# One shared last pass: the fourth kan of the last two units as a pair with full rows, and their stores on two DMA queues

## The chip, the cores and the metric

The kernel runs on one core of a Trainium2 chip. The metric is the device time of one execution, in microseconds (us). The core has a matrix engine (PE), a vector engine (DVE), a scalar engine (ACT) that evaluates functions, a general engine (POOL), and a synchronising engine (SP) that here issues DMAs. DMAs are issued from SP, ACT or POOL into a queue of that engine and carried out by 16 DMA engines. Work on the engines runs side by side; each engine takes its own instructions strictly in the order in which they were written.

## What is computed

The input x is 16 images of 32 channels of 128 x 128 in float32. There are two layers, each a group norm followed by a block whose result is added to its input:

```python
x = x + _L0_conv_ref(_gn(x), ...)     # layer 0: attention over channels, heads are 8 images
x = x + _L1_conv_ref(_gn(x), ...)     # layer 1: windows of 8 x 8, four "fastkan" layers

def _fastkan(x, ln_g, ln_b, ws, wb, bb):
    ln = _layernorm(x, ln_g, ln_b)
    basis = jnp.exp(-((ln[..., None] - GRID) / DENOM) ** 2)      # 8 bumps per value
    return basis.reshape(...) @ ws.T + jax.nn.silu(x) @ wb.T + bb
# in layer 1, y = _layernorm(windows):
a = _fastkan(y seen along the rows, k1...)
d = _fastkan(y seen along the columns, k2...)
e = _fastkan(y, k3...)
z = _fastkan(a + d + e, k4...)
out = z + wins
```

The fourth kan (k4) works on the sum of the first three, so for one piece of the image it can't begin before the third is complete.

## The kernel before

**Units.** Layer 0 needs sums over whole images: the kernel first loads x, turns it on DVE (L658) and sums a Gram matrix on PE (L684). From it `attention` works out one small matrix per half of the batch (L697 to L974). After that, layer 0 is only a matrix product per piece. The image is cut into 64 units of 128 partitions x 1024 values, numbered n = 0 to 63 (N = 64). Layer 1 is done unit by unit.

**Passes.** The four kans are run in pairs, since a kan fills only half of a tile that is 2048 values wide. Pass a of unit n holds kan 1 and kan 2 of that unit. Pass b of unit n holds kan 3 of unit n in its first half and kan 4 of unit n - 2 (BACK = 2) in its second half. Weights and norm scales lie accordingly: in `wt_b` (L418) and `back["b"]` (L416) the upper 64 partitions hold k3 and the lower 64 hold k4, and likewise in the columns `par_b` (L327), built in `parameters` (L486 to L585) at the start from 8 DMAs on POOL's queue (L508) and small operations on DVE. Since kan 4 lags by two, pass b is run N + BACK = 66 times. In passes 64 and 65 there is no kan 3 left, so `norm_b` (L1266) puts the one z into both halves; kan 3's half of the result is thrown away.

One pass is a chain:
- `norm`: 16 matmuls subtract the mean (L1110 through `tiled`, L436), ACT copies to SBUF (L1115, two halves), squares (L1118), PE averages (L981), ACT makes the inverse root (L983, L984), PE spreads it over the partitions (L1123).
- `scale`: DVE multiplies, two halves (L1140).
- `seed`: ACT makes the first bump (L1149, L1154) and two ratios R, up and down (L1151, L1157).
- `ladder`: DVE makes the other seven bumps by multiplying with R, one after the other in each direction (L1169, seven operations).
- `products`: PE multiplies each bump with its weights, 16 matmuls of 32 x 32 at a time (L436), sums them in a pair of PSUM tiles X, and adds the silu blocks (L1205; `silus`, L1300, after the fourth bump) and, for kan 3, the results of kans 1 and 2 (L1314 to L1331).

Kan 3's sum is copied out by ACT as z (`evict_z`, L1251), and ACT makes its silu (`silus`, L1068, L1083, with a load of the function table before, and another after at L1084). Kan 4's sum is added to the unit's input by DVE (`result`, L1351), which needs the unit's xh loaded again (`again`, L1370), and `store` (L1355 to L1364) writes it by four DMAs on SP's queue. The columns and the rows are exchanged between kans by DMAs on SP's queue too: `move` (L1098, `d<-yy`) and `move_back` (L1241).

**What sets the order.** The functions named above are generators. A small planner, `Flow` (L87 to L236), runs them when the kernel is built. It knows each step's engine, an assumed cost and the buffers that the step takes, and writes out the instructions in the order in which it would start them. For the steady part the order on each engine is written out by hand (`ORDER`, L53 to L74, a list of step names with the distance in units); the start, before the second Gram matrix is complete, and the tail are left to the planner's assumed times. Tiles come from pools with few buffers (L450 to L471; two xh, two z, two X, two Y), so a step can also wait for a buffer.

Of the kernel before, what the change touches and what calls it, by code (L numbers as in the profile page):

```python
# [10 lines left out]
F32 = mybir.dt.float32  # L11
AF = mybir.ActivationFunctionType
ALU = mybir.AluOpType
# [6 lines left out]
P = 128  # L20
NG = 8
NT = NG + 1
# [23 lines left out]
LAG = 0.2  # L46
LANDING = 2.5
PATIENCE = 3.0
BACK = 2
# [190 lines left out]
def conv_preact_kernel(  # L240
# [75 lines left out]
    def column():  # L316
        used[0] += 1
        return vec[:, used[0] - 1 : used[0]]
# [6 lines left out]

    par_a = [column() for _ in range(4)]
    par_b = [column() for _ in range(4)]  # L327


    quad = const.tile([P, 4], F32, name="quad")  # L330
# [82 lines left out]
        )  # L413


    back = {name: const.tile([P, P], F32, name=f"back_{name}") for name in ("0", "a", "b")}  # L416
    wt_a = const.tile([P, NT, 32], F32, name="wt_a")
    wt_b = const.tile([P, NT, 32], F32, name="wt_b")  # L418

    silu_a = [const.tile([P, P], F32, name=f"silu_a{k}") for k in range(2)]  # L420
    silu_b = [const.tile([P, P], F32, name=f"silu_b{k}") for k in range(2)]
# [22 lines left out]
    def layers():  # L444
        with ExitStack() as es:
# [40 lines left out]
            def parameters():  # L486

                yield "get", "projections"
                raw, = yield step("POOL", 85.0, "sz")
                back_t = raw[:, 0:384].rearrange("p (k q m) -> p k q m", k=3, q=4)  # L490
                st_a = [
                    raw[:, 384 + k * NT * 16 : 384 + (k + 1) * NT * 16].rearrange("p (t n) -> p t n", t=NT)
                    for k in range(2)
                ]
                st_b = [raw[:, 704 + k * 32 : 736 + k * 32] for k in range(2)]
# [9 lines left out]
                for q in range(4):  # L505
                    for s in range(2):
                        at = q * 32 + s * 16
                        nc.gpsimd.dma_start(  # L508
                            out=wt_b[at : at + 16, :, :], in_=(w3 if q < 2 else w4)[s * 64 : s * 64 + 16]
                        )  # L510
                        for k, src in enumerate((w3, w4)):
                            nc.gpsimd.dma_start(
                                out=st_b[k][at : at + 16, :], in_=src[s * 64 : s * 64 + 16, NG, :]
                            )
# [4 lines left out]
                for par, top, bottom in (  # L519
                    (par_a, (c1["k1_g"], c1["k1_b"]), (c2["k2_g"], c2["k2_b"])),  # L520
                    (par_b, (cr["k3_g"], cr["k3_b"]), (cr["k4_g"], cr["k4_b"])),
                ):
                    g, bq, bp_, bn = par
                    yield step("DVE", 0.8)
                    for o, (mine_g, mine_b) in ((slice(0, 64), top), (slice(64, 128), bottom)):
                        TS(g[o, :], mine_g[o, :], INV_DENOM, None, ALU.mult)
                        TS(bq[o, :], mine_b[o, :], INV_DENOM, 0.5, ALU.mult, ALU.add)
                        TS(bp_[o, :], mine_b[o, :], 2.0 * INV_DENOM, None, ALU.mult)
                        TS(bn[o, :], mine_b[o, :], -2.0 * INV_DENOM, None, ALU.mult)
                for k, (name, groups, scale) in enumerate(  # L530
                    (
                        ("0", quad, cr["pn_g"]),
                        ("a", group8.rearrange("p q j -> p (q j)"), par_a[0]),
                        ("b", quad, par_b[0]),
                    )
                ):
                    n = 8 if name == "a" else 4
                    t = back_t[:, k]
                    yield step("DVE", 0.2)
                    TS(t[:, :, 0:n], groups.unsqueeze(1).to_broadcast([P, 4, n]), scale, None, ALU.mult)  # L540
                    ps_, = yield step("PE", 0.4, "Y")
                    nc.tensor.transpose(ps_[:, 0, 0:P], t.rearrange("p q m -> p (q m)"), ident)
                    yield step("DVE", 0.3)
                    nc.vector.tensor_copy(back[name], ps_[:, 0, 0:P])
                    give("Y")


                for k in range(2):
# [20 lines left out]
                        group8[:, :, 1].unsqueeze(2).unsqueeze(3).to_broadcast([P, 4, 2, 8]),  # L569
                        ALU.mult,  # L570
                    )
                yield step("DVE", 0.45)
                TT(wt_b, wt_b, fac.unsqueeze(2).to_broadcast([P, NT, 32]), ALU.mult)
                for k in range(2):
                    yield step("DVE", 0.5)
# [529 lines left out]
            def norm(name, n, wt, rhs, e, then):  # L1105
# [11 lines left out]
                sq, = yield step("ACT", 1.81, "u")  # L1117
                ACT(sq, v, AF.Square)  # L1118
                lr = yield from rsqrt_rows(sq, P, e, 4, "lr")
                give("u")  # L1120
                rb = yield step("PE", 1.1, "Y", "Y")
                for q in range(4):
                    MM(  # L1123
                        rb[q // 2][:, q % 2, :],
                        lhsT=back[name][32 * q : 32 * q + 32, :],
                        rhs=lr[32 * q : 32 * q + 32, :],
                        start=True,
                        stop=True,
                    )
# [125 lines left out]
            def norm_a(n):  # L1255
# [7 lines left out]
                    lambda: used(("d", n), "d", 2),  # L1263
                )

            def norm_b(n):  # L1266
                y = z = None
                if n < N:
                    y = yield "get", ("yy", n)
                if n >= BACK:  # L1270
                    z = yield "get", ("z", n - BACK)
                rows = lambda t, h: t[:, 4 * h : 4 * h + 4, 0, :]
                cols = lambda t, h: t[:, 512 * h : 512 * h + 512]
                two = (y, rows) if n < N else (z, cols), (z, cols) if n >= BACK else (y, rows)

                def then():
                    if n < N:
                        used(("yy", n), "yy", 3)
                    if n >= BACK:
                        used(("z", n - BACK), "z", 2)  # L1280

                yield from norm(
                    "b",
                    n,
                    c32,
                    lambda g_, q: two[q // 2][1](two[q // 2][0], q % 2)[32 * g_ : 32 * g_ + 32],
                    e4m,
                    then,
                )

            def pair_b(n):
# [3 lines left out]

                def bank(acc, at, rows, k, h):
                    to = acc[k][at : at + rows, h, :]
                    return to.rearrange("p (h n w) -> p h w n", h=4, w=8) if k else to

                def silus(acc):  # L1300
                    for k, (key, m) in enumerate((("s", n), ("sz", n - BACK))):
                        if 0 <= m < N:
                            t = yield "get", (key, m)
                            yield step("PE", 1.06, lag=0.0)
                            cols = lambda h, o: t[o, 512 * h : 512 * h + 512]
                            third = lambda h, o: cols(h, o).rearrange("p (h w n) -> p h w n", h=4, w=8)
                            blocks(
                                lambda h: silu_b[k],
                                third if k else cols,
                                lambda h, f: bank(acc, 64 * ((f + h) % 2), 64, k, h),  # L1310
                            )
                            used((key, m), key, 1)

                def adds(acc):  # L1314
                    ar = yield "get", ("ad", n)
# [17 lines left out]
                also = {2: silus}  # L1333
                if n < N:
                    also[5] = adds
                acc = yield from products("b", n, wt_b, also, (0, 2, 0, 2), bank)
                if n < N:
                    put(("z_acc", n), acc[0], LAG)
                else:
                    give("X")  # L1340
                if n >= BACK:
                    put(("last", n - BACK), acc[1], LAG)
                else:
                    give("X")

            def result(n):
# [8 lines left out]
            def store(n):  # L1355
                bp, kk, j = units[n]
                xh = yield "get", ("result", n)
                yield step("SP", 2.6, lag=0.0)
                for b in range(4):
                    nc.sync.dma_start(  # L1360
                        out=out_rows[bp * KK + kk, b, :, :, j * RB : (j + 1) * RB], in_=xh[32 * b : 32 * b + 32, :]
                    )
                late = fl.moved(1.4, 2.0)
                give("xh", late)  # L1364
# [5 lines left out]
                nc.sync.dma_start(out=xh, in_=xd)  # L1370
                put(("again", n), xh, fl.moved(1.4))

            both = [("b", n) if b else ("a", n) for n in range(N + BACK) for b in range(2) if b or n < N]
            one = lambda name, task: [(name, 0, task)]
            every = lambda name, task, units=N: ((name, n, task(n)) for n in range(units))
            with tc.manual_schedule(engines=IN_ORDER):
# [10 lines left out]
                        every("evict_z", evict_z),  # L1387
                        every("result", result),
                        every("again", again),
                        every("scale_b", lambda n: scale("b", n), N + BACK),  # L1390
                        every("scale_a", lambda n: scale("a", n)),
                        ((f"seed_{k}", n, seed(k, n, par_a if k == "a" else par_b)) for k, n in both),
                        every("norm_b", norm_b, N + BACK),
                        every("norm_a", norm_a),
                        every("silus", silus, N + LATE),
                        every("move_back", move_back),
# [92 lines left out]
```

## Time and profile before

| what | us |
|---|---|
| median of 3 runs | 2868.09 (2866.86 to 2873.42) |
| the profiled execution | 2870.64 |
| its span, from first to last instruction | 2868.9 |
| PE busy | 2746.1 (96%) |
| DVE busy | 2685.3 (94%) |
| ACT busy | 2517.7 (88%) |
| POOL busy | 53.8 (2%) |
| the last operation on DVE (`result` of unit 63, L1351) ends | 2854.9 |

The span divides into a start up to some 330 us (loads, Gram matrices, attention, the first units), a steady stretch in which a unit follows a unit, and a tail. Groups of instructions that matter here: the ladder, L1169, 910 operations of 2286 ns; the products, L436, 605 ns for a matmul record, several of which run beside each other on parts of the array; L1140, 260 of 1216 ns; L1115, 260 of 1015 ns; L1118, 1905 ns; L1149 to L1157, 1901 to 1996 ns each; the eviction of z, L1251; the stores, 256 DMAs of 128 KB on SP's queue. A name such as `u<-R,u` in these views gives the tile written and the tiles read. "PEclk" or "granted clock" is the share of its full clock that PE was granted in a stretch.

### The profile page before, as it was taken

What the parts mean: (1) busy time and instruction counts of PE and PEld (TensorE: products, weight loads), DVE (VectorE), ACT (ScalarE), POOL (GpSimd) and SP (SyncE); (2) the same over time, 40 slices, a digit from 0 to 9 for tenths busy, and PEclk for the clock granted to TensorE, in tenths of its full rate; (3) what the DMA queues carried; (4) which work ended last, traced back from release to release, by engine and by line L of the source; (5) the groups of instructions that cost most, each with busy time, mean ns of one, the idle gap of its engine ahead of it and who ended that gap; (6) DMA issues with size and microseconds to landing.
All of it is one profiled execution on the core that took longest, in us unless ns stands there. A gap on an engine that the chain in (4) does not pass through costs nothing.

```text
span 2868.9 us, 100690 instructions
## 1 busy us (share of the span) xinstructions
PE 2746.1 (96%) x45955; PEld 1091.5 (38%) x45955; DVE 2685.3 (94%) x1793; ACT 2517.7 (88%) x2035; POOL 53.8 (2%) x109
## 2 busy tenths in 40 slices
PE   6999999999999999999999999999999999999985
PEld 6874433333333333333333333333333333333321
DVE  4747999999999999999999999999999999999986
ACT  0026899999999999999999999999999999999973
POOL 4200000000000000000000000000000000000000
PEclk9999999999999999999999999999999999999987
DMA  9652233333333333333333333333333333333311
GB/s 243 179 123 60 75 113 110 105 104 113 113 103 98 108 109 116 116 101 110 103 116 113 94 111 100 116 114 108 108 106 111 114 97 103 108 109 114 102 56 35
DMA packets 206152, 311.04 MB, mean 108 GB/s; under 512 B 24480, under 2 KB 156064, under 8 KB 205728
## 3 DMA queue, kind: packets, MB, share of 16 engines
q1 hardware_dynamic: 192512, 285.29, 33.8%
q10 hardware_dynamic: 9504, 16.85, 2.4%
q8 instruction: 362, 5.93, 0.9%
q0 software_dynamic: 3712, 2.46, 0.4%
q14 instruction: 62, 0.51, 0.1%
HBM read 103.18 MB, written 67.11 MB: 59 GB/s over the span
## 4 chain that ended last, share of the span: by engine, by line
PE 64%; DVE 20%; issue 6%; ACT 4%; DMA 4%; SPq 1%; DVEq 0%; ACTq 0%
PE X L436 25%; DVE u L1169 14%; PE X L1205 10%; PE Y L1004 7%; PE Y L436 4%; PE Y L1019 4%; PE X L1324 4%; PE X L684 3%; DVE yc L1140 3%; PE Y L1123 2%; PE Y L981 2%; DVE yy L1057 2%; DMA u<-in_x 1%; SPq L1241 1%; ACT u L1118 1%
## 5 line engine op out<-in xcount | busy, mean ns | idle before, releaser
L1169 DVE SCALAR_TENSOR_TENSOR u<-R,u 128x2048 f32<-128x2048 f32 x910 | 2043.4, 2286 | 38.0 <-ACT u L1154 17.0
L436 PE MATMUL X<-u,wt_a 32*32 32x512 f32 x16384 | 663.8, 605 | 11.2 <-ACT u L1154 4.1
L436 PE MATMUL X<-u,wt_b 32*32 32x512 f32 x16896 | 638.3, 605 | 16.3 <-ACT u L1154 9.4
L436 PEld LDWEIGHTS X<-u,wt_a 32*32 32x32 f32 x16384 | 302.7, 103 | 289.1 <-issue 136.4
L436 PEld LDWEIGHTS X<-u,wt_b 32*32 32x32 f32 x16896 | 224.7, 103 | 384.3 <-issue 194.2
L1140 DVE TENSOR_TENSOR yc<-yc,Y 128x1024 f32<-128x1024 f32 x260 | 305.4, 1216 | 10.6 <-PE Y L1123 7.5
L1149 ACT ACTIVATE u<-yc,vec 128x2048 f32<-128x2048 f32 x130 | 258.5, 1989 | 29.6 <-DVE yc L1140 24.7
L1115 ACT ACTIVATE yc<-Y 128x1024 f32<-128x1024 f32 x260 | 250.2, 1015 | 35.5 <-DMA u<-in_x 22.9
L1004 PE MATMUL Y<-x,pt 128*128 128x512 f32 x512 | 236.7, 605 | 31.5 <-DVE yc L1140 31.5
L1157 ACT ACTIVATE R<-yc,vec 128x2048 f32<-128x2048 f32 x130 | 259.5, 1996 | 2.5 <-DVE u L1169 1.5
L1151 ACT ACTIVATE R<-yc,vec 128x2048 f32<-128x2048 f32 x130 | 258.8, 1991 | 0.0
L1118 ACT ACTIVATE u<-yc 128x2048 f32<-128x2048 f32 x130 | 247.6, 1905 | 2.9 <-DVE u L1169 2.2
L1154 ACT ACTIVATE u<-u 128x2048 f32<-128x2048 f32 x130 | 247.1, 1901 | 0.0
L684 PE MATMUL X<-R 128*64 128x257 f32 (+3 forms) x2048 | 154.4, 312 | 22.8 <-DVE R L658 22.1
L983 ACT ACTIVATE lr<-Y,vec 128x512 f32<-128x512 f32 (+1 forms) x194 | 131.3, 677 | 45.0 <-PE Y L981 45.0
L1004 PEld LDWEIGHTS Y<-x,pt 128*128 128x128 f32 x512 | 92.2, 190 | 179.9 <-issue 92.9
L684 PEld LDWEIGHTS X<-R 128*64 128x64 f32 x2048 | 143.4, 142 | 42.3 <-DVE R L658 23.8
L981 PE MATMUL Y<-u,e 128*32 128x512 f32 x1040 | 139.6, 604 | 3.3 <-ACT u L1118 3.3
L1233 ACT ACTIVATE ad<-X,col 128x1024 f32<-128x1024 f32 x128 | 134.0, 1095 | 1.7 <-PE X L436 1.7
L1019 PE MATMUL Y<-xh,c 128*128 128x512 f32 x256 | 127.0, 618 | 2.4 <-ACT xh L1014 2.4
L984 ACT ACTIVATE lr<-lr 128x512 f32<-128x512 f32 (+1 forms) x194 | 122.4, 631 | 6.2
L1205 PE MATMUL X<-sd,silu_a 64*64 64x512 f32 x1024 | 124.7, 602 | 0.0
(210 smaller groups left out, 2472.9 us busy)
## 6 DMA issues: line engine op xcount, KB each, us to landing
xh<-xh SPq DMA_DIRECT2D x128, 512.0 KB
d<-yy SPq DMA_DIRECT2D x512, 128.0 KB
ad_r<-ad SPq DMA_DIRECT2D x512, 128.0 KB
x<-in_x SPq DMA_DIRECT2D x32, 1024.0 KB
out<-xh SPq DMA_DIRECT2D x256, 128.0 KB
u<-in_x SPq DMA_DIRECT2D x28, 256.0 KB
u<-in_x ACTq DMA_DIRECT2D x28, 256.0 KB
ad<-in_x SPq DMA_DIRECT2D x14, 256.0 KB
```

Of the source, the lines that this page charges most:

```text
L436: MM(dst(to, g_), lhsT=wt[32 * g_ : 32 * g_ + 32, :], rhs=rhs(g_, (to - turn[g_]) % 4), start=start, stop=stop,)
L684: MM(g[64 * q : 64 * q + 64, k, lo:hi], lhsT=t[:, b, at : at + 64], rhs=t[:, b, lo:hi], start=first, stop=last,)
L1004: MM(xp[:, u, :], lhsT=pts[bp][:, k, kk * P : (kk + 1) * P], rhs=xr[:, k, u * 512 : (u + 1) * 512], start=k == 0, stop=k == KK - 1,)
L1115: ACT(v[:, i * RB : (i + 1) * RB], flat(yt[i]), AF.Identity)
L1118: ACT(sq, v, AF.Square)
L1140: TT(v[:, o], v[:, o], flat(rb[i]), ALU.mult)
L1149: ACT(u, v, AF.Square, bias=bq)
L1151: ACT(up, v, AF.Exp, bias=bp_, scale=2.0)
L1154: ACT(u, u, AF.Exp, scale=-1.0)
L1157: ACT(down, v, AF.Exp, bias=bn, scale=-2.0)
L1169: STT(t, by, BIG, tiles[at[way]], ALU.min, ALU.mult)
L1205: MM(dst(i, f), lhsT=wt(i)[o, o], rhs=rhs(i, o), start=False, stop=False)
```

## The change

Three things change in the code.

1. The last two runs of pass b become one. Pass b is run N + 1 = 65 times. In run 64 the first half holds kan 4 of unit 62 and the second half kan 4 of unit 63 (`fourths`). It takes z of both units, the silu of both, and gives two results.
2. This run needs k4's weights in all partitions, so the start builds a second set: columns `par_z`, scales `back["z"]`, weights `wt_z` (8 more DMAs on POOL's queue, 8 more column operations, one more transpose on PE with its copy, one more product on DVE). The planner is told 0.9 instead of 0.45 us for the step that scales the weights, and gets one more step each for the columns and the transpose.
3. The stores of units 62 and 63 are issued alternately on SP's and on ACT's queue, two DMAs on each.

```diff
+    par_z = [column() for _ in range(4)]
...
-    back = {name: const.tile([P, P], F32, name=f"back_{name}") for name in ("0", "a", "b")}
+    back = {name: const.tile([P, P], F32, name=f"back_{name}") for name in ("0", "a", "b", "z")}
...
+    wt_z = const.tile([P, NT, 32], F32, name="wt_z")
...
+                        nc.gpsimd.dma_start(out=wt_z[at : at + 16, :, :], in_=w4[s * 64 : s * 64 + 16])
...
+                    (par_z, (cr["k4_g"], cr["k4_b"]), (cr["k4_g"], cr["k4_b"])),
...
+                        ("z", quad, par_z[0]),
...
-                yield step("DVE", 0.45)
+                yield step("DVE", 0.9)
+                TT(wt_z, wt_z, fac.unsqueeze(2).to_broadcast([P, NT, 32]), ALU.mult)
...
+                scales = back["z" if n == N else name]
...
+            def fourths(n):
+
+                return [m for m in ((n - BACK, n - BACK + 1) if n == N else (n - BACK,)) if m >= 0]
+
             def norm_b(n):
...
+                ins = ([("yy", n)] if n < N else []) + [("z", m) for m in fourths(n)]
+                two = []
+                for kind, m in ins:
+                    t = yield "get", (kind, m)
+                    two.append((t, rows if kind == "yy" else cols))
...
                 def silus(acc):
...
+                    ins = [("s", n)] if n < N else []
+                    for k, (key, m) in enumerate(ins + [("sz", m) for m in fourths(n)]):
...
-                acc = yield from products("b", n, wt_b, also, (0, 2, 0, 2), bank)
...
+                acc = yield from products("b", n, wt_z if n == N else wt_b, also, (0, 2, 0, 2), bank)
+                outs = ([("z_acc", n)] if n < N else []) + [("last", m) for m in fourths(n)]
+                for key, t in zip(outs, acc):
+                    put(key, t, LAG)
...
+                queues = (nc.sync, nc.scalar) if n >= N - 2 else (nc.sync, nc.sync)
                 for b in range(4):
-                    nc.sync.dma_start(
+                    queues[b % 2].dma_start(
                         out=out_rows[bp * KK + kk, b, :, :, j * RB : (j + 1) * RB], in_=xh[32 * b : 32 * b + 32, :]
                     )
...
-                        every("scale_b", lambda n: scale("b", n), N + BACK),
+                        every("scale_b", lambda n: scale("b", n), N + 1),
...
-                        every("norm_b", norm_b, N + BACK),
+                        every("norm_b", norm_b, N + 1),
```

In the order of instructions that the planner writes for the changed kernel, the steady stretch is the same on every engine. In the start the order differs (on PE up to row 1385 of some 11,900, on DVE up to row 375 of 1,761, on ACT and SP correspondingly), and in the tail run 65 is gone and run 64 stands after the last z.

More of the change, by code (lines that the diff above doesn't have):

```diff
@@ L489, in parameters @@
                 raw, = yield step("POOL", 85.0, "sz")
-                back_t = raw[:, 0:384].rearrange("p (k q m) -> p k q m", k=3, q=4)
+                back_t = raw[:, 0:512].rearrange("p (k q m) -> p k q m", k=4, q=4)
                 st_a = [
-                    raw[:, 384 + k * NT * 16 : 384 + (k + 1) * NT * 16].rearrange("p (t n) -> p t n", t=NT)
+                    raw[:, 512 + k * NT * 16 : 512 + (k + 1) * NT * 16].rearrange("p (t n) -> p t n", t=NT)
                     for k in range(2)
                 ]
-                st_b = [raw[:, 704 + k * 32 : 736 + k * 32] for k in range(2)]
+                st_b = [raw[:, 832 + k * 32 : 864 + k * 32] for k in range(2)]
                 for k, src in enumerate((w1, w2)):
@@ L1124, in norm @@
                         rb[q // 2][:, q % 2, :],
-                        lhsT=back[name][32 * q : 32 * q + 32, :],
+                        lhsT=scales[32 * q : 32 * q + 32, :],
                         rhs=lr[32 * q : 32 * q + 32, :],
@@ L1264, in norm_a @@
                 )
+            def fourths(n):
+                return [m for m in ((n - BACK, n - BACK + 1) if n == N else (n - BACK,)) if m >= 0]
             def norm_b(n):
[L1267 to L1271, printed above, removed]
                 rows = lambda t, h: t[:, 4 * h : 4 * h + 4, 0, :]
                 cols = lambda t, h: t[:, 512 * h : 512 * h + 512]
-                two = (y, rows) if n < N else (z, cols), (z, cols) if n >= BACK else (y, rows)
+                ins = ([("yy", n)] if n < N else []) + [("z", m) for m in fourths(n)]
[3 more added lines that the diff above has]
+                    two.append((t, rows if kind == "yy" else cols))
                 def then():
[L1277 to L1280, printed above, removed]
+                    for kind, m in ins:
+                        used((kind, m), kind, 3 if kind == "yy" else 2)
+                if len(two) == 1:
+                    two = two * 2
                 yield from norm(
@@ L1297, in bank @@
                     to = acc[k][at : at + rows, h, :]
-                    return to.rearrange("p (h n w) -> p h w n", h=4, w=8) if k else to
+                    return to.rearrange("p (h n w) -> p h w n", h=4, w=8) if k or n == N else to
                 def silus(acc):
[L1301 to L1312, printed above, removed]
+                    ins = [("s", n)] if n < N else []
+                    for k, (key, m) in enumerate(ins + [("sz", m) for m in fourths(n)]):
+                        t = yield "get", (key, m)
+                        yield step("PE", 1.06, lag=0.0)
+                        cols = lambda h, o: t[o, 512 * h : 512 * h + 512]
+                        third = lambda h, o: cols(h, o).rearrange("p (h w n) -> p h w n", h=4, w=8)
+                        blocks(
+                            lambda h: silu_b[1 if n == N else k],
+                            third if k or n == N else cols,
+                            lambda h, f: bank(acc, 64 * ((f + h) % 2), 64, k, h),
+                        )
+                        used((key, m), key, 1)
                 def adds(acc):
@@ L1335, in pair_b @@
                     also[5] = adds
-                acc = yield from products("b", n, wt_b, also, (0, 2, 0, 2), bank)
[L1337 to L1343, printed above, removed]
+                acc = yield from products("b", n, wt_z if n == N else wt_b, also, (0, 2, 0, 2), bank)
+                outs = ([("z_acc", n)] if n < N else []) + [("last", m) for m in fourths(n)]
+                for key, t in zip(outs, acc):
+                    put(key, t, LAG)
+                for _ in range(2 - len(outs)):
                     give("X")
@@ L1371, in again @@
                 put(("again", n), xh, fl.moved(1.4))
-            both = [("b", n) if b else ("a", n) for n in range(N + BACK) for b in range(2) if b or n < N]
+            both = [("b", n) if b else ("a", n) for n in range(N + 1) for b in range(2) if b or n < N]
             one = lambda name, task: [(name, 0, task)]
@@ L1389, in layers @@
                         every("again", again),
-                        every("scale_b", lambda n: scale("b", n), N + BACK),
+                        every("scale_b", lambda n: scale("b", n), N + 1),
                         every("scale_a", lambda n: scale("a", n)),
-                        ((f"seed_{k}", n, seed(k, n, par_a if k == "a" else par_b)) for k, n in both),
-                        every("norm_b", norm_b, N + BACK),
+                        ((f"seed_{k}", n, seed(k, n, par_a if k == "a" else par_z if n == N else par_b)) for k, n in both),
+                        every("norm_b", norm_b, N + 1),
                         every("norm_a", norm_a),
```

## The prediction

> **What bounds the kernel now.** I read the share of busy time over the span first, then the chain that ended last, then its final 220 us with the engines' timelines, then the start.
>
> From the page, part 2 (tenths of busy time in 40 slices of 71.7 us):
> ```profile
> PE   6999999999999999999999999999999999999985
> DVE  4747999999999999999999999999999999999986
> ACT  0026899999999999999999999999999999999973
> ```
> From slice 5 on three engines are full together. So the middle is a fixed beat: the built instruction order of the changed kernel is the same there on every engine (the last differing row of VectorE (DVE) is its 375th of 1,761, until the tail begins), and a shift of the start shifts the end one for one. Only the start (to about 330 us) and the tail (from about 2780 us) can change.
>
> The chain of work that ended last, window 2650 to 2870 (start, us, what):
> ```profile
> 2805.15 2.00 ACT u L1149
> 2807.16 1.00 ACT z L1251
> ...
> 2811.88 8.91 DVE u L1169 x4
> ...
> 2830.07 2.00 ACT u L1149
> ...
> 2851.67 1.92 PE X L436 x32
> 2853.59 0.02 issue
> 2853.61 1.28 DVE xh L1351
> ```
> The last z of the third kan (unit 63) is ready at 2808.2. Pass b64 (unit 62 twice) holds DVE until 2827.7, pass b65 (unit 63 twice) ends with its result at 2854.9. But the span ends at 2868.9. What fills those 14.0 us:
> ```profile
> 2831.25 26.61 SPq L1360 DMA_DIRECT2D out<-xh  x8
> ```
> ```profile
> 2832.00:2843.00 11.00, 6.26 (x113) 1.12 (x128) 7.21 (x4) 5.66 (x4) 0.00 (x0) 0.56 0.13 47
> 2856.00:2867.00 11.00, 0.00 (x0) 0.00 (x0) 0.00 (x0) 0.00 (x0) 0.00 (x0) 0.50 0.13 47
> ```
> (SyncE's (SP's) DMA queue; then stretches with PE, PEld, DVE, ACT, POOL, granted clock, DMA share, GB/s.) A store of one unit is 4 DMAs of 128 KB. All four together keep 0.13 of 16 engines busy, that is two, at 47 GB/s: 512 KB take 11 us (0.52 MB / 47 GB/s). Unit 62's store (2832 to 2843) lies beside pass b65; unit 63's lies bare.
>
> **Tail, step by step.**
> *Removed:* pass b65 with its 7 ladder steps (15.8 us of DVE), and L1115, L1118, L983/L984, L1123, L1140 and L1149 to L1157 once. *Moved:* the norm of pass b64 now waits for z of unit 63. Behind that wait on PE and ScalarE (ACT) stands only the same pass.
> - z earlier. Before, pass b64's square (L1118) held up the `ad` eviction until 2789.19 though PE was through at 2788.24; its L1123 (1.07) held PE's next-to-last product; its L1149 held the z eviction from 2806.26 to 2807.06. Without them PE ends unit 63 at about 2805.95, z is there at 2807.05: 1.1 earlier.
> - From z to the scaled values. ACT's new order has the silu of z first: table load 1.28, silu 1.06, load 1.28, to 2810.7 (the norm's matmuls, 1.15, lie beside it). L1115 twice 1.92, L1118 1.91: 2814.6. PE has then idled 6.3 us; after 6.8 idle us before 2835.8 the granted clock was 0.50 and 32 products took 2.02 instead of 1.15. So I take L981 at 1.95 for 1.07 and L1123 at 2.09 (its row at 2773.24): 2816.6, L983/L984 1.35, 2818.0, L1123 to 2820.1. The second L1140 ends at 2821.5 (were PE warm: 1.9 less).
> - From there as before: scaled at 2830.05, result at 2854.89 is 24.84 us. Result of unit 62 at 2846.35, of unit 63 at 2847.5. The second silu block (1.09) falls into PE's waits for the ladder (1.05 to 1.24 each). So the final store starts 8.5 earlier. (Its buffer is no limit: `again` of unit 63 needs one of the two xh tiles, free when unit 61's store has landed, about 2819, and takes some 3 us.)
> - The store is now 1 MB, since nothing is left to cover unit 62's 512 KB. No row shows these DMAs on two queues. Bounds: if ACT's two DMAs run on other engines than SP's, the 14.0 us stay and the tail gains 8.5; if on the same two, 512 KB more at the steady rate (mean 51.9 GB/s in the 1 us stretches from 2859 on) cost 10.1. Between 186 and 200, where loads on two queues meet `d<-yy`, 16 engines are full (share 1.05) at 208 GB/s, against 241 with loads alone: a second queue brought no bandwidth beyond full engines. I take the same two: +10.1. Issue (0.75 each) gets shorter, but isn't the limit.
>
> The Trainium skill speaks against the two queues: its page "DMA: Bandwidth & Descriptors" says in "Why a DMA increments its semaphore by 16 and not by 1" that the slowest dimension of the pattern sets the number of engines and that the lowest-numbered ones are taken, and in "Issuing engines are not separate DMA queues" that SP and ACT feed the same 16. The pattern here is 2x16x1024, so by the page 2 engines for all eight DMAs, and the sum as I take it; the trace shows the two engines for SP, and nothing of ACT.
>
> Tail: -8.5 + 10.1 = **+1.6** (-0.3 with a warm PE).
>
> **Start.** Added: 8 GpSimd DMAs (24 took 87.65 to 105.4, so 0.74 each, +5.9; they land near 116, first read after L864, 131 before: cover 15 us), on DVE 8 column operations (0.06 apart), L540, L544 and the wt_z product: 0.5+0.2+0.25+0.45 = 1.4, a transpose on PE, 0.33. DVE is busy 13 to 17 of 20 us there, so this hides. What counts is that the planner, with these steps, orders the start anew:
> 1. wt_a's building (L551 to L566, 4 us) no longer stands before L831. Before, PE waited 2.1 for it (at 119.2) and then ran L837 in 3.66 instead of 1.98. With the new transpose some 3 us gained.
> 2. The move of unit 0 (`d<-yy`) now comes after the last gram loads on SP. The rows of before (SP's queue, then who PE waited for):
> ```profile
> 182.95 9.61 SPq L1098 DMA_DIRECT2D d<-yy  x8
> 192.66 2.51 SPq L637 DMA_DIRECT2D u<-in_x  x4
> ```
> ```profile
> PE Y L436 <- DMA d<-yy: 6.3, 1, 6.3
> ```
> PE met norm a0 at 190.4 and waited 6.3. Now 72 more gram matmuls (4.5 steps at 2.34 = 10.5 us) stand before norm a0, and the loads go first. So the wait is filled: norm a0 at about 199, the gram sum done near 212 instead of 221.8. That is 3 + 6.3 earlier, less small waits, with L981 and L1123 of b0 (2.1) and two more steps put off.
> 3. Given back: seed a0 now stands on ACT behind attention(1)'s copies, b0's square and the second xh. Counted from the gram's end: z of attention to L811 15.6, DVE L826 17.4, L1057 and L1140 19.8, L1149 21.8, L1014 23.0, L983/L984 24.2, L1151 26.1, L1154 28.3: first product 28 after the gram's end against 22.9 before (244.73 - 221.8). The last ladder step of a0 ends at +46.5 (before +38.4), its product at +49.5: 261.5 against 267.0, with L852 (1.2) already done. Then a 1.1 wait for the softmax.
> Sum of the start: -6.7 + 1.1, rounded to **-5**. Bounds: -9 if nothing is given back, +5 if the gram ends no earlier and the 28 stays.
>
> **Sum:** +1.6 - 5 = -3.4. The profiled execution took 2870.6 (span 2868.9 and 1.7 around it), the median is 2868.1, 2.5 lower; applied to the median: **2864.7** (-0.12%).
>
> **Rivals.**
> - *Other engines for ACT's queue.* For: GB/s would double with idle engines, 14 of 16. Against: four DMAs of one queue already don't spread. -8.5 - 5 = -13.5: 2854.6. 0.13.
> - *Slower: the start loses.* PE in front of unit 0's first product: ACT must finish attention(1)'s steps before seed a0. If the last chunk's loads (2 MB, 9 us at 234 GB/s, sharing with `d`) hold the gram until 221.8 all the same, the product comes 28 after it, +5.1, and +1.6 at the tail: 2874.8. It decides from a gram end later than about 217. For: window 186 to 200 has all DMA engines full. Against: the loads are issued 7 us earlier on SP. 0.13.
> - *The start doesn't move* (fills and delays cancel): 2869.7, and the change doesn't do what it says: a pass removed, no time gained. 0.12.
> - My forecast: 0.62.
>
> **Numbers.** 0.2% (5.7 us) is about what a measurement of this kernel can tell. My forecast (start -9 to +1, tail -0.3 to +1.6): faster 0.20, same 0.41, slower 0.01. Other engines: faster 0.12, same 0.01. Start loses: slower 0.10, same 0.03. Start unmoved: same 0.09, slower 0.03. Together faster 0.32, same 0.54, slower 0.14. Range 2854.5 to 2873.0: from the other-engines case to the start unmoved with some loss; left out are the start's worst and both gains together.
>
> **What would show it.** After the last result, 24 us of stores at DMA share 0.13 (right), or 14 us at 0.25 (rival). Last z to the result of unit 62: 39.3 us, table loads between z and L1115. No 6 us wait of PE for `d<-yy` near 190; attention(1)'s L746 near 212; the first L436 with wt_a 28 after it. Wrong would be a middle that beats differently, or L981 and L1123 at half of my times.

## The result, and the profile after

The changed kernel takes 2878.94 us (median of 5 runs, 2877.36 to 2882.2) beside 2868.09 (5 runs) of the kernel before. The ratio is 1.0042, with a 95% interval of 1.003 to 1.0053: **slower by 11 to 12 us**, where the prediction had 3.4 faster. The profiled execution took 2881.57, its span 2879.5.

Lines of the code have moved: in the changed kernel the products are L438 (before L436), norm's copies L1121, its square L1124, its spread L1130 (before L1123), `scale` L1147 (L1140), the seed L1156 to L1164, the ladder L1176 (L1169), z's eviction L1258, the result L1359, the stores L1370. Attention's steps are L697 to L980, those met below L745 to L837, and `layer0_norm` is L1010 to L1071 with its row average in L987.

The changed kernel's page, part 2, has the same shape as before:

```profile
PE   6998999999999999999999999999999999999973
DVE  4746899999999999999999999999999999999983
ACT  0026799999999999999999999999999999999962
```

The plateau is full in both, and its beat is the same: from one `result` to the next 39.6 us in every kernel of this study. So what moved lies at the two ends.

**The tail.** The chain of work that ended last in the changed kernel (start, us, what):

```profile
2813.36 1.11 ACT z L1258
...
2820.12 1.92 ACT u L1124
...
2835.79 8.91 DVE u L1176 x4
...
2851.67 2.14 PE X L438 x32
```

and what follows it, from its timeline and a window over the store (window, PE, PEld, DVE, ACT, POOL, granted clock, DMA share, GB/s):

```profile
2855.14 2.96 SPq L1370 DMA_DIRECT2D out<-xh  x4
2855.15 3.85 ACTq L1370 DMA_DIRECT2D out<-xh  x4
```
```profile
2856.00:2878.00 22.00, 0.00 (x0) 0.00 (x0) 0.30 (x1) 0.00 (x0) 0.00 (x0) 0.50 0.12 48
```

There is one ladder where the last 60 us held two. Unit 62's result ends at 2855.1 (unit 63's 1.2 later), and the span ends at 2879.5, 24.4 after it. In these 22 us both queues together keep 0.12 of 16 engines busy, that is two, at 48 GB/s, the rate of SP's queue alone before.

To compare the tails without the start, count from the ladder in which the kernels still agree: it begins at 2777.82 before and at 2785.19 after, **7.4 later**. From there to the end of the span the changed kernel needs 94.3 us and the one before 91.1: the tail loses 3.2. So 7.4 of the 10.6 us between the two spans were lost before the tail began.

**The start.** `result` of unit 6 ends the start conveniently: it begins at 624.2 before and at 630.2 after. Whom PE waited for between 180 and 240 us in the changed kernel (engine, what waited, releaser: us, times, longest):

```profile
PE Y L438 <- DMA d<-yy: 1.4, 1, 1.4
PE Y L987 <- ACT u L799: 1.4, 1, 1.4
PE Y L1010 <- DVE yy L1063: 1.3, 1, 1.3
PE Y L745 <- ACT xh L1020: 1.3, 1, 1.3
PE Y L768 <- ACT xc L1034: 1.2, 1, 1.2
PE Y L786 <- DVE u L780: 1.1, 1, 1.1
PE Y L1058 <- DVE u L820: 1.0, 1, 1.0
...
```

The wait for `d<-yy` has shrunk from 6.3 to 1.4, as predicted. In its place stand many waits of about 1 us each, all of them at products that write a tile Y (the tiles for PE's short steps) and spread over the steps of attention(1) and the second `layer0_norm`. In the PE timeline of the changed kernel (start, us, engine, line, what, count, idle before):

```profile
211.53 3.70 PE L1010 MATMUL Y<-x,pt 128*128 128x512 f32 x8
...
232.94 2.08 PE L1058 MATMUL Y<-lr,back 32*128 32x512 f32 x4 [0.97 <-DVE u L820]
236.33 5.51 PE L1010 MATMUL Y<-x,pt 128*128 128x512 f32 x8 [1.31 <-DVE yy L1063]
...
250.43 1.14 PE L438 MATMUL X<-u,wt_a 32*32 32x512 f32 x32
```

The sum of the second Gram matrix is done at 211.5, when L1010 starts ("the gram's end" from here on), 10.3 earlier than before (221.8), again as predicted. But the first product with `wt_a` comes 38.9 us after that, at 250.4, instead of 22.9 after (244.7). And the second L1010, the same eight matmuls as the first, takes 5.51 instead of 3.70.

One thing in VectorE's timeline of the changed kernel explains why so many steps wait for Y:

```profile
210.25 1.22 DVE L1147 TENSOR_TENSOR yc<-yc,Y 128x1024 f32<-128x1024 f32 x1 [5.36 <-PE Y L1130]
...
236.19 1.21 DVE L1147 TENSOR_TENSOR yc<-yc,Y 128x1024 f32<-128x1024 f32 x1
```

These are the two halves of `scale` of unit 0's pass a. Each half frees one Y tile, and there are two Y tiles. In the kernel before, both halves ran back to back (2.31 us from 208.69). Here the planner has put 21 operations of attention(1) and the second `layer0_norm` between them, so that for 26 us one Y tile is held by data that are ready, and all of PE's other work runs through the other tile.

### The profile page after: what moved, and what is told of

It is laid out like the page before. It is cut to its first block, busy times and chain, and to the rows that moved or that the text cites. A ratio compares the mean times of both kernels' runs of the same rounds, so it can differ in the third digit from the quotient of the medians.

```text
span 2879.5 us, 100088 instructions
## 1 busy us (share of the span) xinstructions
PE 2737.3 (95%) x45652; PEld 1085.5 (38%) x45652; DVE 2668.8 (93%) x1795; ACT 2505.9 (87%) x2026; POOL 57.7 (2%) x117
## 4 chain that ended last, share of the span: by engine, by line
PE 61%; DVE 20%; issue 6%; ACT 5%; DMA 5%; SPq 1%; DVEq 0%; POOL 0%; ACTq 0%; POOLq 0%
PE X L438 24%; DVE u L1176 15%; PE X L1212 10%; PE Y L1010 7%; PE Y L438 4%; PE Y L1025 4%; PE X L1335 4%; DVE yc L1147 3%; PE Y L1130 2%; PE Y L987 2%; DVE yy L1063 2%; PE X L690 1%; DMA col<-in_cols 1%; DMA sz<-in_w 1%; SPq L1248 1%
## 5 line engine op out<-in xcount | busy, mean ns | idle before, releaser
L1176 DVE SCALAR_TENSOR_TENSOR u<-R,u 128x2048 f32<-128x2048 f32 x903 | 2027.6, 2286 | 30.3 <-ACT u L1161 14.2
L438 PE MATMUL X<-u,wt_a 32*32 32x512 f32 x16384 | 658.3, 600 | 12.8 <-DVE u L1176 4.3
L438 PE MATMUL X<-u,wt_b 32*32 32x512 f32 x16384 | 614.1, 599 | 2.8 <-ACT ad L1240 1.7
L438 PEld LDWEIGHTS X<-u,wt_a 32*32 32x32 f32 x16384 | 299.6, 103 | 291.3 <-issue 143.9
L438 PEld LDWEIGHTS X<-u,wt_b 32*32 32x32 f32 x16384 | 218.9, 103 | 353.5 <-issue 193.1
L1147 DVE TENSOR_TENSOR yc<-yc,Y 128x1024 f32<-128x1024 f32 x258 | 303.4, 1216 | 31.0 <-PE Y L1130 28.0
L1156 ACT ACTIVATE u<-yc,vec 128x2048 f32<-128x2048 f32 x129 | 256.5, 1988 | 23.0 <-DVE yc L1147 18.4
L1121 ACT ACTIVATE yc<-Y 128x1024 f32<-128x1024 f32 x258 | 248.5, 1017 | 26.8 <-PE Y L438 26.6
L1010 PE MATMUL Y<-x,pt 128*128 128x512 f32 x512 | 240.0, 612 | 32.4 <-DVE yc L1147 30.7
L1164 ACT ACTIVATE R<-yc,vec 128x2048 f32<-128x2048 f32 x129 | 257.4, 1995 | 2.8 <-DVE u L1176 1.8
L1124 ACT ACTIVATE u<-yc 128x2048 f32<-128x2048 f32 x129 | 245.7, 1905 | 4.7 <-DVE u L1176 3.5
L1010 PEld LDWEIGHTS Y<-x,pt 128*128 128x128 f32 x512 | 93.4, 192 | 184.1 <-issue 95.0
L690 PEld LDWEIGHTS X<-R 128*64 128x64 f32 x2048 | 142.7, 141 | 38.8 <-DVE R L664 23.6
L987 PE MATMUL Y<-u,e 128*32 128x512 f32 x1032 | 139.3, 608 | 9.9 <-ACT u L1124 9.9
```

Source lines behind the costliest of these rows:

```text
L438: MM(dst(to, g_), lhsT=wt[32 * g_ : 32 * g_ + 32, :], rhs=rhs(g_, (to - turn[g_]) % 4), start=start, stop=stop,)
L690: MM(g[64 * q : 64 * q + 64, k, lo:hi], lhsT=t[:, b, at : at + 64], rhs=t[:, b, lo:hi], start=first, stop=last,)
L1010: MM(xp[:, u, :], lhsT=pts[bp][:, k, kk * P : (kk + 1) * P], rhs=xr[:, k, u * 512 : (u + 1) * 512], start=k == 0, stop=k == KK - 1,)
L1121: ACT(v[:, i * RB : (i + 1) * RB], flat(yt[i]), AF.Identity)
L1147: TT(v[:, o], v[:, o], flat(rb[i]), ALU.mult)
L1156: ACT(u, v, AF.Square, bias=bq)
```

## The experiments

**Theory A:** the planner's new order of the start costs the time, through that held Y tile: PE's chain runs on one tile, and PE, often waiting, runs at a lower clock. The added work costs nothing, and the tail costs 2 to 3. **Rival B:** ScalarE's order alone decides, since it must finish attention(1)'s steps before the seed of a0. **Rival C:** the eight added DMAs and the operations on DVE and PE delay the start themselves. For the tail, the question was what the store is bound by.

All times below are medians; each ratio is to runs of the kernel before on the same chip (24 runs, median 2866.04, for the first four kernels; 17 runs, 2866.38, for the last four).

| kernel | us | ratio to before | 95% interval |
|---|---|---|---|
| the change | 2878.94 | 1.0042 | 1.003 to 1.0053 |
| e1_plan_kept | 2871.23 | 1.0019 | 1.0008 to 1.0031 |
| e7_setup_alone | 2874.52 | 1.0025 | 1.0014 to 1.0037 |
| e6_a0_whole | 2868.62 | 1.0010 | 1.0001 to 1.0019 |
| e2_one_queue | 2878.74 | 1.0035 | 1.0022 to 1.0049 |
| e8_whole_spread | 2852.63 | 0.9957 | 0.9944 to 0.997 |
| e9_whole_spread_one | 2852.65 | 0.9956 | 0.9942 to 0.9969 |
| e5_before_spread | 2859.96 | 0.9980 | 0.997 to 0.999 |
| e4_kept_spread | 2852.84 | 0.9962 | 0.9946 to 0.9977 |

### The added work without the new order: e1_plan_kept

```diff
-                    yield step("DVE", 0.8)
+                    if par is not par_z:
+                        yield step("DVE", 0.8)
...
+                    if name == "z":
+                        continue
+                    with_z = [(0, name, t, scale)]
+                    if name == "b":
+                        with_z.append((1, "z", back_t[:, 3], par_z[0]))
...
+                    for u, _, t, scale in with_z:
+                        nc.tensor.transpose(ps_[:, u, 0:P], t.rearrange("p q m -> p (q m)"), ident)
...
-                yield step("DVE", 0.9)
+                yield step("DVE", 0.45)
```

> The change, with its added setup work kept out of the planner's sight: the fourth set's columns, transpose and products stand inside existing steps at their old assumed costs, so the start has the order of the kernel before on every engine, plus only the added instructions. Pass 64 and the two queues stay as in the changed kernel. Theory A (the planner's new order of the start costs about 7, the added work itself nothing): the first product with wt_a back near 245 us (changed kernel 250.4, before 244.7), the last eviction of z back near 2806, and only the tail's 3.3 left: about 2871.6. Rival C (the added DMAs and operations themselves delay the start): first product still near 250, about 2878.

Measured: ratio 1.0019, some 5 us over before (2 to 9), and by the two ratios 6.6 under the changed kernel. The first product comes at 245.4 and the last z's eviction ends at 2805.0. The added DMAs, columns, transpose and product are all in this kernel, so rival C falls: they hide. What is left over the kernel before is of the size of the tail's loss (3.2 in the profiles above).

### The new order without the merged pass: e7_setup_alone

```diff
+    par_z = [column() for _ in range(4)]
...
+    wt_z = const.tile([P, NT, 32], F32, name="wt_z")
...
+                        ("z", quad, par_z[0]),
...
-                yield step("DVE", 0.45)
+                yield step("DVE", 0.9)
+                TT(wt_z, wt_z, fac.unsqueeze(2).to_broadcast([P, NT, 32]), ALU.mult)
```

> The kernel before, with passes 64 and 65 and the stores untouched, and only the changed kernel's setup: the second weight set is built by the same steps and used by nothing. The start then has the changed kernel's order. If the start's order alone carries the loss (theory A): first product near 250.4, the middle shifted by 6 to 7, total 2874 to 2876. If the loss came from the merged pass and its stores: 2868.

Measured: 1.0025, 7 us over before (4 to 11). The second half of a0's scaling again runs 27 us after the first (204.40 and 231.83), and the first product comes 40.5 after the gram's end. In this profile the gram ended 6 us earlier than in the changed kernel's (205.7), so it comes at 246.2 and not at 250.4 as I expected; the distance from the gram's end is what repeats. Setting up weights that nothing uses thus costs some 60% of what the whole change costs (0.0025 of 0.0042).

### The held tile freed: e6_a0_whole

```diff
+                whole = (name, n) == ("a", 0)
+                if whole:
+                    yield step("DVE", 2.28)
                 for i in range(2):
                     o = slice(i * RB, (i + 1) * RB)
-                    yield step("DVE", 1.14, lag=0.0 if i == 0 else None)
+                    if not whole:
+                        yield step("DVE", 1.14, lag=0.0 if i == 0 else None)
```

> The changed kernel with one edit: both halves of the scaling of unit 0's pass a are planned as one step, so that on VectorE the second half stands directly behind the first (in the changed kernel it is 26 us later and holds one of the two Y tiles for 28 us). The orders on PE and on SP are the same, and ScalarE's differs by one swap. Theory A (the held Y tile makes the chain of attention(1) run on one tile, PE waiting and running at a low clock): first product 4 to 8 us earlier, 2871 to 2875. Rival B (ScalarE alone, whose seed of a0 stands behind attention(1)'s steps, sets the time): no change, 2878 to 2880.

Measured: 1.0010, **9 to 10 us under the changed kernel** (by the ratios and by the medians), more than the 4 to 8 expected. Its waits of PE from 180 to 240 us, then its PE timeline:

```profile
PE Y L438 <- DMA d<-yy: 1.5, 1, 1.5
PE Y L1010 <- DVE yy L1063: 1.3, 1, 1.3
...
PE Y L786 <- DVE u L780: 0.9, 1, 0.9
PE Y L1025 <- ACT xh L1020: 0.9, 1, 0.9
...
```
```profile
211.85 3.70 PE L1010 MATMUL Y<-x,pt 128*128 128x512 f32 x8
...
228.83 3.70 PE L1010 MATMUL Y<-x,pt 128*128 128x512 f32 x8 [1.33 <-DVE yy L1063]
...
241.23 2.01 PE L438 MATMUL X<-u,wt_a 32*32 32x512 f32 x32
```

The gram ends at the same time as in the changed kernel, but the first product comes 29.4 after it instead of 38.9. The 9.5 us can be added up from the two PE timelines, between the first L1010 and the end of the second. Waits of PE: 8.3 in the changed kernel (eight, of 0.25 to 1.38 each), 3.2 here; that is 5.1. The same matmuls at a lower clock: L786 2.92 against 1.78, L987 1.92 against 1.34, L1058 2.08 against 1.19, L1010 5.51 against 3.70; that is 4.4. The clock is seen in one window (columns as above), first the changed kernel, then e6:

```profile
228.00:236.00 8.00, 5.26 (x16) 2.74 (x14) 2.72 (x9) 3.57 (x5) 0.00 (x0) 0.50 0.00 0
```
```profile
228.00:236.00 8.00, 6.01 (x26) 2.20 (x26) 4.66 (x14) 4.61 (x5) 0.00 (x0) 1.00 0.26 68
```

Rival B falls: ScalarE has the same order (but for one swap, a copy of 0.6 ahead of a square of 1.06, which can account for 1 us at most) and seed a0 still stands behind attention(1), yet 9.5 are gone. Nor was it that the seed itself lacked its data: in e6 its first step runs at 227.2, and the next still waits on ScalarE until 234.9 behind the copies of the second L1010. PE's chain was late, and ScalarE with it.

Of the two parts, the waits repeat and the clock does not. Between the two L1010, the waits of PE add up to 8.1 to 8.3 in the three kernels that hold the tile and to 3.2 to 3.6 in the three that free it. But with the tile freed the second L1010 took 3.70 in e6, 5.40 in e8 and 6.25 in e9, so the 4.4 for the clock is the figure of one pair of profiles.

How firm this is over several profiles, grouped by the order of the start (times of one profile each, in us):

| order of the start | gram's end to first product | first product | `result` of unit 6 |
|---|---|---|---|
| before's (before, e1, e4, e5) | 22.9, 24.6, 24.6, 21.3 | 244.7, 245.4, 243.5, 244.1 | 624.2, 621.3, 621.3, 621.3 |
| the change's (after, e2, e7) | 38.9, 38.8, 40.5 | 250.4, 250.7, 246.2 | 630.2, 636.5, 628.1 |
| with a0 whole (e6, e8, e9) | 29.4, 29.4, 31.8 | 241.2, 238.9, 239.6 | 620.8, 621.1, 619.8 |

The change's order stands apart in every column, narrowly in the second (246.2 against 245.4), and the other two differ clearly in the first two. By unit 6 the change's order has lost 9.6 on average, 4.7 of it before the first product. The granted clock over 212 to 350 is lower there too (0.85 to 0.90, against 0.95 to 0.98 and 0.93 to 0.94).

The traces also show where the other 5 arise: in the second ladder (pass b of unit 0). There VectorE meets L903, a step of attention that needs PE's L893 (before: L897, L887). In the order of before it stands ahead of the ladder's last step, in the new order ahead of the last but one, and it waits. First the kernel before, then the changed one:

```profile
287.82 0.61 DVE L897 TENSOR_SCALAR pt<-Y,u 128x128 f32<-128x128 f32 x2 [0.72 <-PE Y L887]
```
```profile
293.50 0.61 DVE L903 TENSOR_SCALAR pt<-Y,u 128x128 f32<-128x128 f32 x2 [6.38 <-PE Y L893]
```

This wait is 0.7 in all four kernels with before's order, 6.4 to 6.9 with the change's and 5.2 to 5.7 with a0 whole. The last step of that ladder starts at 288.7 on average with before's order, at 299.5 with the change's and at 288.6 with a0 whole. So freeing the Y tile mends the first loss, and the new order keeps the second. No run changes the place of L903 alone, so this second cause is read from the traces and not tested.

### One queue for the stores: e2_one_queue

```diff
-                queues = (nc.sync, nc.scalar) if n >= N - 2 else (nc.sync, nc.sync)
+                queues = (nc.sync, nc.sync)
```

> The changed kernel with all eight stores of the last two units on SP's queue. If the two queues use the same two DMA engines, as the DMA share of 0.12 to 0.13 and 48 to 53 GB/s after the last result say: the same time as the changed kernel within 1 us (2878 to 2880). If ScalarE's queue had brought engines of its own: 1 MB on one pair takes some 10 us more, about 2888.

Measured: 1.0035, the same as the change within both intervals. After the first result (ends 2858.5) its store takes 24.0 us, against 24.4 on two queues:

```profile
2858.59 6.91 SPq L1370 DMA_DIRECT2D out<-xh  x8
```
```profile
2860.00:2882.00 22.00, 0.00 (x0) 0.00 (x0) 0.00 (x0) 0.00 (x0) 0.00 (x0) 0.50 0.12 47
```

Same share, same rate. The second queue brought nothing that shows.

### The stores spread: e8_whole_spread and e9_whole_spread_one

```diff
-                    queues[b % 2].dma_start(
-                        out=out_rows[bp * KK + kk, b, :, :, j * RB : (j + 1) * RB], in_=xh[32 * b : 32 * b + 32, :]
-                    )
+                    for s in range(2) if n >= N - 2 else ():
+                        queues[s].dma_start(
+                            out=out_rows[bp * KK + kk, b, s, :, j * RB : (j + 1) * RB],
+                            in_=xh[32 * b + 16 * s : 32 * b + 16 * s + 16, :],
+                        )
...
```

> The changed kernel with unit 0's scaling of pass a planned whole (as in e6_a0_whole) and the stores of the last two units cut into eight DMAs of 16 rows each, so that their slowest dimension is 16 instead of 2, four on each of the two queues. If the slowest dimension sets how many DMA engines a store uses (the changed kernel showed two engines, 0.13 of 16, for eight DMAs on two queues), the last store spreads over all 16 engines and is then limited by issue, 8 on each queue at 0.74 to 0.96 us: the end comes 9 to 11 us after the first result of pass 64 instead of 24.4, DMA share well over 0.13, and the kernel is 13 to 15 us under e6_a0_whole, that is 10 to 12 under before (ratio about 0.996). If the number of engines has another cause: as e6_a0_whole, ratio 1.001.

> The same as e8_whole_spread, but all 16 stores on SP's queue. If with spread engines the issue is the limit, one queue needs 16 issues at 0.75 to 0.86 us, 12 to 14 us, and the end comes 15 to 17 us after the first result: 5 to 7 us slower than e8_whole_spread, still 7 to 9 faster than e6_a0_whole. If the second queue brings nothing: the same as e8_whole_spread.

The pattern of one DMA goes from 2x16x1024 to 16x1024; bytes and addresses are the same. The issues and the windows of e8 (first result ends at 2842.2, span 2849.7):

```profile
2842.27 4.13 SPq L1375 DMA_DIRECT2D out<-xh  x8
2842.28 4.30 ACTq L1375 DMA_DIRECT2D out<-xh  x8
```
```profile
2842.00:2844.00 2.00, 0.00 (x0) 0.00 (x0) 1.44 (x2) 0.00 (x0) 0.00 (x0) 1.00 0.51 92
2844.00:2846.00 2.00, 0.00 (x0) 0.00 (x0) 0.00 (x0) 0.00 (x0) 0.00 (x0) 0.51 0.74 242
2846.00:2848.00 2.00, 0.00 (x0) 0.00 (x0) 0.00 (x0) 0.00 (x0) 0.00 (x0) 0.50 0.67 191
```

The megabyte is out 7.5 us after the first result instead of 24.4, at a share of up to 0.74 and 242 GB/s, and the kernel is 0.0053 in ratio (15 us) under e6. Share 0.13 was two engines and the slowest dimension was 2; with 16, most engines work. The packets in the traces say the same. In the changed kernel exactly two data packets ran at once for 20.4 of the store's 21.4 us; in e8 twelve or more did for 3.6 of its 4.8. The number of DMAs doubled too, from 8 to 16, but four of the old shape (before) and eight (the changed kernel, e2) had kept the same share of 0.12 to 0.13, so it was not the number. That is how the Trainium skill has it (page "DMA: Bandwidth & Descriptors", section "Why a DMA increments its semaphore by 16 and not by 1": the slowest dimension of a pattern fixes the number of engines used, 16 at most), and these runs agree with it.

On one queue (e9) 16 issues take 7.30 us and the end comes 10.2 after the first result. In the two profiles the store is thus 2.7 shorter with the second queue, now that it has engines to feed; the medians, 2852.65 and 2852.63, don't show it, and their intervals are too wide to exclude it. My price of 5 to 7 was too high, since a DMA of 16 rows is issued in 0.46 us and not in the 0.75 to 0.86 of one of 32.

### Spreading without merging, and merging with the old order: e5_before_spread, e4_kept_spread

The edit of e5 is the last diff on the kernel before; e4 is e1's and that diff on the changed kernel.

> The kernel before, passes 64 and 65 as they were, with only the stores of the last two units cut into DMAs of 16 rows on the two queues. Unit 63's store then takes 4 issues on each queue (3 to 4 us) and some 2.5 to land instead of 14.0: about 8 us under before (ratio 0.9972). If spreading does nothing: 1.000.

> e1_plan_kept (the merged pass with the order of the start kept) with the stores spread as in e8_whole_spread. Spreading takes 13 to 15 us from e1_plan_kept's time, which stood 5 us over before: 8 to 10 us under before (ratio 0.9965 to 0.997). Against e5_before_spread it shows what the merged pass is worth by itself once the store no longer eats it: I expect 2 to 5 us in favour of the merged pass, since its last result is ready some 8 us earlier and its store is twice as long.

Measured: e5 0.9980 (6 us under before, 3 to 9); unit 63's result ends at 2852.0 and the span at 2857.2, 5.2 later instead of 14.0. The saving is 8.8 there; 1.2 of it goes at ScalarE, where the first four stores' issue (1.80 us) stands between two steps of pass 65's seed, and the ladder waits 5.72 instead of 4.57. e4 is at 0.9962. Side by side, e4 is 7.1 us under e5 by the medians, 5 by the ratios (whose intervals overlap a little), and 6.2 by the two profiles, counted from the result of unit 6 (2229.6 and 2235.9 to the end); I had expected 2 to 5. **So merging the pass is worth some 5 to 7 us once the store is spread,** and with two engines the bare megabyte ate more than that.

## Why the prediction was wrong

- **What bounds the kernel:** right. The plateau beats at 39.6 us in every kernel, and shifts of the start reach the end.
- **Start, step 1** (`wt_a` not before L831): right. PE's 2.1 us wait is gone and the matmuls behind it took 1.99 instead of 3.66. A new wait of 1.4 (L812, for a copy at L549 ahead of it on Y) takes part of that back.
- **Start, step 2** (the wait for `d<-yy` filled, norm a0 at about 199, gram's end near 212): right; 1.4, 199.9, 211.5.
- **Start, step 3 is the step that failed:** "first product 28 after the gram's end". It was 38.9. My list already had the second L1140 at 19.8, late, and I took it only as an input of the seed. I did not ask what else it held: one of two Y tiles, from 210 to 237. So the chain I had timed from rows with two Y tiles and PE at full clock ran on one tile, with PE waiting at nearly every step and at half clock. The first checkpoint already shows it: L811 (now L817), which I had put at 15.6, ended 20.9 after the gram. Without the held tile, e6 gives 29.4: the 28 was the right size for the order I had in mind, not for the order on the page. In place of -5 the start gave +6.0 by unit 6 and +7.4 by the last common ladder, and my bound of +5 had left the tile out as well. The chain behind the first product was too short too: I allowed 1.1 for a wait behind a0's ladder, and VectorE's wait at L903 alone grew from 0.72 to 6.38. (The sum itself, -6.7 + 1.1, is -5.6, which I wrote as -5.)
- **Tail:** right in mechanism, a little small in size. The store took 24.4 against the 24.1 of my sum; L987 1.93 and L1130 2.09 against 1.95 and 2.09. Missed: the first half of the scaling began only when all eight L1130 were over (L1147 starts at 2827.68), some 1.1 us. The term +1.6 measured +3.2 in the changed kernel's profile, and +2.7 over all profiles with unspread stores, from `result` of unit 6 to the end (four merged kernels 2247.3 on average, the kernel before and e7 2244.6).
- **Rivals.** *Other engines for ACT's queue:* refuted, by the share of 0.12 and by e2. *Slower: the start loses:* the side was right, the mechanism wasn't. It was to decide from a gram end later than 217, and the gram ended at 211.5. *The start doesn't move:* refuted by `result` of unit 6, 6.0 later, and by e7.
- **What stays open:** even with the tile freed, the 4.5 us by which the first product is earlier (239.9 against 244.4 on average) have shrunk to 1.4 by unit 6. They are gone at the second ladder's last step (288.6 against 288.7), behind the wait at L903; what they would be worth with L903 in its old place was not run. Open too is how much of the loss at the first product is the clock's: 4.4 in one pair, and not the same in others.

## What to carry to other kernels

When a reordering puts a consumer late, price not only what waits for its result but also the buffer that it keeps: with two tiles, one held tile turns every step between other engines into a visible wait. A planner that starts steps by assumed times can pay for an unrelated step that is added far away, so compare the new order at the scarce pools, not only at the queues. And before work is removed in front of a bare final transfer, make that transfer use all its engines; here the shape of the DMA was worth 15 us, and the second queue nothing at the old shape and nothing that the medians show at the new one.

## What I had not expected of the hardware

- **PE at half clock though it never idled long.** In the changed kernel the granted clock is 0.50 in every 2 us window from 224 to 240, while PE is busy 66% of the stretch 228 to 236 and no wait on its timeline there is over 1.4 us. It returns to 1.00 there after the second L1010 had run for some 4 us without a break. In the Trainium skill, page "TensorE: Matmul & The Clock Gate", the clock drops after an idle window of about 3.4 us (Part 1, "What's actually happening") and micro-idling between groups of matmuls is named as a second way to lose it ("A second HAM failure mode: psum-queue depth-cycling"). The waits here are all short, so this trace has the like of the second. The kernel before, with both Y tiles in use, had 0.99 or 1.00 in six of the eight such windows from 224 to 240, 0.50 in one and 0.66 in one. Short waits are not the whole of it, though: in e9, with the tile free, the clock is 0.50 in three windows from 218 to 224 in which PE counts as busy all of the time. What brings it down and back is not shown here.
- **With two engines the second queue's packets start late.** In the changed kernel the first packets of SP's queue start at 2856.4 and those of ACT's at 2860.3, though both issued at 2855.1. With the stores spread (e8) they are 0.4 us apart (2843.1 and 2843.5).
- **The same busy share of the DMA engines can mean half the rate.** In e9 one queue moved 131 GB/s at a mean share of 0.76 (2844 to 2852); in e8 two queues reached 242 at 0.74 (2844 to 2846). The packets differ: one of 4096 bytes took 159 ns (median) with two engines at work in the changed kernel, 159 on ACT's and 244 on SP's queue in e8, and 368 in e9. Why they get longer is not shown.
